# Sorted attention on one core: the second group's rows fetched between the rotations of the first group's queries, and gates and second latents in column groups of TensorE

## The chip, the core and the metric

One core of a Trainium2 chip runs the whole program. The metric is the device time of one execution in microseconds (us), as the median of several executions. The core has five engines that run beside each other, each with a queue of its own: TensorE (PE, matrix products; its weight loads are listed as PEld), VectorE (DVE), ScalarE (ACT), GpSimd (POOL) and SyncE (SP). In this kernel SP issues the plain DMA transfers, and POOL issues every indirect transfer (one whose rows are picked by a list of indices) besides arithmetic of its own.

## What is computed

Two layers on `x` of 16 x 256 tokens x 512, all in fp32, each an attention-like part and an ffn, each with a residual. Cut to what matters:

```python
x = x + L0_xattn(layernorm(x), k, fside_S2_0, ctx)   # long convolution, gated
x = x + L0_ffn(layernorm(x), ...)                    # 8 routed experts, top 2, and a shared one
x = x + L1_xattn(layernorm(x), ctx, itok, ...)       # latent attention
x = x + L1_ffn(layernorm(x), ...)                    # 512 -> 2048 -> gelu -> 512

# L0_ffn, the routing
logits = xf @ gate_w                                 # (tokens x 512) @ (512 x 8)
top_logits, top_idx = top_k(logits, 2)

# L1_xattn
q_c = q @ W_dq                                       # 512 -> 192 latents
q_nope = (q_c @ W_uq)                                # 16 heads of 128
q_rope = rope(q_c @ W_qr)                            # 16 heads of 64, rotated by position
scores = (q_nope . k_nope + q_rope . k_rope) * scale
good = (k_ids <= itok) & (k_ids >= itok - 8)         # 9 keys per token at most
out = softmax(where(good, scores, -1e30)) @ v @ W_o
```

There are 4096 tokens. Each token has an id `itok`, and it sees only the keys from `itok - 8` to `itok`.

## The kernel before

**Stages.** The kernel (class `Kernel`) runs five stages after each other: `conv_shared` (the convolution, the gate logits, the routing and the shared expert; PE ends it at about 982 us), `routed` (71 tiles of 128 rows through the routed experts, to about 1302 us), `attention_sorted` (to about 2260 us), `ffn` (to the end), and a fallback that isn't run on this input. A matmul in fp32 is recorded as two instructions ("passes").

**The convolution.** `conv_shared` loops over 32 rows, h = 0 to 31, with two convolution halves in each. A half is 20 passes of 512 columns (`y`, L292), which DVE multiplies with the context (`pr`, L297) and reduces (`oT`, L304). For each row `turn_inputs` transposes the values on PE (`pvt`, L258) into a PSUM buffer that the row before has used, and so it waits until DVE's products of that row (`kv`, 4 per half, `product`, L274) are done; PE turns the result (`po`, L316, and `xT`/`xt`, L317). Everything else of the stage is hung in between by four lists of steps per half (`one`, `mid`, `two`, `end`), which a schedule written by hand keeps in this order on PE, DVE and ACT. Four rows make one group of 512 tokens (`T4`, q = h % 4). At q = 0 the group that was completed a row before gets its gate logits: `logits` (L375, matmul at L380) is hung in `end`, and computes for each of 4 token tiles the product of 4 slices of `xT` (128 x 128, the stationary side) with a slice of `w_gate` (128 x 8, the moving side). That is 16 matmuls of 8 columns, or 32 passes, in each of 7 groups (h = 4, 8, ..., 28); the last group of tokens follows behind the loop, by the same function. At q = 1 DVE picks the two best experts from them (`tops`). On DVE the sort of the tokens by id also runs in this stage (`ranks`, L639 to L644, at h = 3 to 18).

**Sorted attention.** The tokens, sorted by key id, are cut into 32 tiles of 128, T = 0 to 31, and these into 8 groups of four (g = T // 4, t = T % 4). What a tile needs is spread over these functions:

- `fetch` brings a tile's rows of x (`xt`) and of the rotation's sines and cosines (`rr`), `fetch_routed` its two rows of routed experts (`yt`, twice), and `fetch_keys` its windows of keys (`gw`, 4 times). All are indirect DMAs that POOL issues (`fetch_rows`, L1727).
- `tokens` adds the two `yt` to `xt` on DVE (L1407 to L1410), normalizes (`layernorm`: L66, L68 on DVE, L70 and L71 on POOL, `xh` at L72 on DVE), and turns `rr` and `xh` on PE (L1416; `pt`, L99; copied by ACT at L100).
- `latents` (L1424) computes the 192 latents of a group of 512 tokens: two products of 128 latents each, `q0` (0 to 127) and `q1` (128 to 191, which stand in `q1` twice, in its lower and in its upper 64 lines, since the weights hold these 64 columns twice), 4 matmuls of 512 columns each, copied by ACT (L1428).
- `heads` is called 4 times per group, for 2 pairs of heads each time: products with `q0`, then with `q1` (L1439 to L1450), then the rotation: ACT swaps halves (`sw`, L1455), DVE multiplies by one factor (L1457), POOL multiplies and adds (L1458, L1459).
- `window` turns the keys on PE (`pkw` L1472, `prw` L1477) and makes the mask on DVE; `scores` (L1500, L1506), `weigh` and `weights` (DVE, with Exp on ACT) and `values` (`pu`, L1544) are the attention itself; `project` multiplies by W_o (`po`, 32 passes, L1560), DVE adds it to `xt` (L1565), and POOL sends the tile off (`x3s`, L1566).

PE's results `pq`, `pqr`, `pqn`, `pkw`, `prw`, `pu`, `po`, `prr` and `pt` share 7 PSUM buffers (tag `m`) in turn. `xt` has 8 buffers, `yt` and `rr` have 4, `gw` has 3.

The main loop, T = 0 to 33, works on tile T and, beside it, prepares the next group: its rows are fetched at t = 0 and 1, its `tokens` follow at t = 0 (tile 0), 1 (tile 1) and 2 (tiles 2 and 3), and at t = 3 come its `latents` and all 4 `heads`. `values` runs one tile behind, `project` two tiles behind. `tc.issue_after(i)` around calls keeps what they issue behind instruction `i` in the order in which the scheduler lays out each engine's queue; before, the one place it names in this stage is `first`, the last normalization of the first group's tokens.

The lines that the change touches are L328 to L329 (`w_gate`), L362 to L384 (`logits`), L745 (where it is hung), L1420 to L1428 (`latents`), L1430 to L1463 (`heads`), L1570 to L1578 (the start of sorted attention) and L1588 to L1629 (the loop's fetches and tokens).

Of the kernel before, what the change touches and what calls it, by code (L numbers as in the profile page):

```python
# [10 lines left out]
F32 = mybir.dt.float32  # L11
I32 = mybir.dt.int32
AF = mybir.ActivationFunctionType
ALU = mybir.AluOpType
# [4 lines left out]
P = 128  # L19
# [3 lines left out]
DC = D // P  # L23
EPS = 1e-5
E, EH, SH = 8, 256, 512
HEADS, HD, R = 16, 128, 64
KVC, QC = 128, 192
# [15 lines left out]
class Kernel:  # L43
# [59 lines left out]
    def conv_shared(self, x1d, xgd):  # L103
        nc, tc, a = self.nc, self.tc, self.a
        with ExitStack() as ctx:
# [4 lines left out]
            wp = pool("ab_w", 1)  # L110
# [214 lines left out]

            def load_shared_weights():
                w = {}
                w["gate"] = wp.tile([P, DC, E], F32, name="w_gate")  # L328
                nc.sync.dma_start(w["gate"], a["gate_w"].rearrange("(c p) e -> p c e", p=P))  # L329
                w["sw1"] = wp.tile([P, DC, SH], F32, name="w_s1")  # L330
                nc.sync.dma_start(w["sw1"], a["sw1"].rearrange("(c p) h -> p c h", p=P))
                w["sb1"] = wp.tile([P, SH // P], F32, name="b_s1")
                nc.sync.dma_start(w["sb1"], a["sb1T"])
                w["sw2"] = wp.tile([P, SH // P, D], F32, name="w_s2")
                nc.sync.dma_start(w["sw2"], a["sw2"].rearrange("(c p) d -> p c d", p=P))
                return w

            def load_experts(c):
# [20 lines left out]
                rows_of, pattern=[[ROOM, E]], base=0, channel_multiplier=0,  # L359
                allow_small_or_imprecise_dtypes=True,  # L360
            )
            T4 = 4  # L362

            def put(index, src):
# [10 lines left out]
            def logits(st, t0, n):  # L375
                xT = st["xT"]
                pl = ps_t.tile([P, n, E], F32, tag="t", name="pl")
                for t in range(n):
                    for c in range(DC):
                        nc.tensor.matmul(  # L380
                            pl[:, t, :], xT[:, c, (t0 + t) * P : (t0 + t + 1) * P], st["w"]["gate"][:, c, :],
                            start=(c == 0), stop=(c == DC - 1),
                        )
                return {"h": st["h"] + t0, "n": n, "pl": pl}  # L384

            def tops(r):

# [327 lines left out]
            w = None  # L715
# [3 lines left out]
            with tc.manual_schedule(engines=order):  # L719
                for h in range(HC):  # L720
# [19 lines left out]
                    if before is not None:  # L740
                        st = before
                        if q == 0:
                            if older is not None:
                                mid.append(lambda: outs(older, 3))
                            end.append(lambda: st.update(r=logits(st, 0, T4)))  # L745
                        elif q == 1:
                            steps = tops(st["r"])
                            one = {k: [steps[k]] for k in range(3)}
                            mid.append(lambda: hidden(st, 0))
                            end += [lambda: rank_rows(st["r"]), lambda: hidden(st, 1)]  # L750
                        elif q == 2:
                            one = {0: [lambda: slots(st["r"])], 1: [lambda: shares(st["r"])]}
                            mid.append(lambda: hidden(st, 2))
                            end.append(lambda: hidden(st, 3))
                        else:
                            mid.append(lambda: outs(st, 0))
                            end += [lambda: outs(st, 1), lambda: outs(st, 2)]
                        if q >= 2:
                            for t in (2 * q - 4, 2 * q - 3):
                                end += [lambda t=t: send(st["r"], t), lambda t=t: send_route(st["r"], t)]  # L760
# [587 lines left out]
    def attention_sorted(self, fetched, ygd, x3s, end_of_queries):  # L1348
# [8 lines left out]
        with ExitStack() as ctx:  # L1357
# [60 lines left out]
                self.transposed(st["xT"][:, :, toks], xh, ps_m, "m")  # L1418

            def latents(st):  # L1420
                for n, lo in (("q0", 0), ("q1", P)):
                    pq = ps_m.tile([P, N], F32, tag="m", name="pq")
                    for c in range(DC):
                        nc.tensor.matmul(  # L1424
                            pq, wdq[:, c, lo : lo + P], st["xT"][:, c, :], start=(c == 0), stop=(c == DC - 1)
                        )
                    st[n] = tp.tile([P, N], F32, tag=n, name=n, bufs=1)
                    nc.scalar.copy(st[n], pq)  # L1428

            def heads(st, two):  # L1430

                q0, q1 = st["q0"], st["q1"]
                pairs = (2 * two, 2 * two + 1)
                lo, hi = slice(0, QC - P), slice(QC - P, P)
                both = (lo, hi)
                pqr = [ps_m.tile([P, N], F32, tag="m", name="pqr") for hp in pairs]
                pqn = [[ps_m.tile([P, N], F32, tag="m", name="pqn") for i in range(2)] for hp in pairs]
                for k, hp in enumerate(pairs):
                    nc.tensor.matmul(pqr[k], wqr0[:, hp * P : (hp + 1) * P], q0, start=True, stop=False)  # L1439
                for k, hp in enumerate(pairs):  # L1440
                    for i in range(2):
                        nc.tensor.matmul(pqn[k][i], m0[:, 2 * hp + i, :], q0, start=True, stop=False)

                for k in range(2):
                    rr = both[k]
                    nc.tensor.matmul(pqr[k], wqr1[rr, two, :], q1[rr, :], start=False, stop=True)
                for k, hp in enumerate(pairs):
                    for i in range(2):
                        rr = both[i]
                        nc.tensor.matmul(pqn[k][i], m1[rr, hp, :], q1[rr, :], start=False, stop=True)  # L1450
                by_chunk = lambda t: t.rearrange("p (c q) -> p c q", q=CQ)
                for k, hp in enumerate(pairs):
                    sw = ap_.tile([P, N], F32, tag="sw", name="sw", bufs=3)
                    for i in range(2):
                        nc.scalar.copy(sw[both[i], :], pqr[k][both[1 - i], :])  # L1455
                    to = qr[:, :, hp * CQ : (hp + 1) * CQ]
                    nc.vector.tensor_tensor(to, by_chunk(pqr[k]), by_chunk(st["rope"][:, 0, :]), ALU.mult)  # L1457
                    nc.gpsimd.tensor_tensor(sw, sw, st["rope"][:, 1, :], ALU.mult)  # L1458
                    nc.gpsimd.tensor_tensor(to, to, by_chunk(sw), ALU.add)  # L1459
                for k, hp in enumerate(pairs):  # L1460
                    for i in range(2):
                        c0 = i * P // 2 + hp * CQ
                        nc.scalar.copy(qn[:, :, c0 : c0 + CQ], by_chunk(pqn[k][i]))  # L1463

            wins = {}

# [101 lines left out]
            new = lambda g: {"g": g, "y": []}  # L1568
            NG = NT_ // T4
            state = {0: new(0)}  # L1570
            for t in range(T4):
                fetch_routed(state[0], t)
                tokens(state[0], t)
            first = self.normed
            latents(state[0])
            window(0)
            for two in range(HP // 2):
                heads(state[0], two)  # L1578
            ats, uts = {}, {}
            for T in range(NT_ + 2):  # L1580
                g, t = T // T4, T % T4
                if T < NT_:
                    if 3 <= T + 2 < NT_:
                        fetch_keys(T + 2)
                    s = scores(state[g], T)
                    e = weigh(T, s)
                    nxt = state.setdefault(g + 1, new(g + 1)) if g + 1 < NG else None
                    if nxt is not None and t < 2:  # L1588
                        with tc.issue_after(first):
                            fetch((g + 1) * T4 + 2 * t)  # L1590
                            fetch_routed(nxt, 2 * t)
                    if nxt is not None and t == 3:
                        latents(nxt)
                if 1 <= T <= NT_:
                    uts[T - 1] = values(T - 1, ats.pop(T - 1))
                if T < NT_:
                    ats[T] = weights(e)
                    if T + 1 < NT_:
                        window(T + 1)
                    if nxt is not None and t == 3:  # L1600
                        for two in range(HP // 2):
                            heads(nxt, two)
                if T >= 2:
                    project(state[(T - 2) // T4], T - 2, uts.pop(T - 2))
                if T == NT_:
# [11 lines left out]
                        self.layernorm(xh, xt, small)  # L1617
                        self.transposed(xT[:, :, k * P : (k + 1) * P], xh, ps_m, "m")
                if T < NT_ and nxt is not None:
                    if t == 0:  # L1620
                        with tc.issue_after(first):
                            fetch((g + 1) * T4 + 1)
                            fetch_routed(nxt, 1)
                    for k in ((0,), (1,), (2, 3), ())[t]:
                        tokens(nxt, k)
                    if t == 1:
                        with tc.issue_after(first):
                            fetch((g + 1) * T4 + 3)
                            fetch_routed(nxt, 3)  # L1629
            return ahead  # L1630
# [261 lines left out]
```

## Time and profile before

| what | value |
|---|---|
| median of 3 timed executions | 3186.18 us (3185.9 to 3187.29) |
| the profiled execution, its own time | 3162.05 us |
| its span, from the first to the last instruction | 3159.9 us |
| mean granted TensorE clock | 0.987 |
| costliest PE groups: convolution L292, project L1560, ffn L1692, ffn L1680 | 572.2, 445.7, 442.0, 385.7 us |
| DVE: pr L297, reduce L304, product L274 | 174.6, 175.6, 174.0 us |
| POOL: indirect fetches of yt, of gw | 71.5, 133.2 us |
| bytes moved | 201.45 MB, 63 GB/s over the span |

The span is cut by the profile into 40 slices of 79 us; in each the PE digit is 9 (90% busy or more), except the first and the last slice (8) and the two around the start of sorted attention, at 1264 to 1422 us (7 and 8). The granted clock has the digit 9 in all but two slices (8, the same two around the start of sorted attention). The chain of work that ended last is followed back only over a last transfer, and holds 0% of the span, so it doesn't tell what bounds the middle. The costliest groups list no idle time of PE above 1.0 us in front of any of their lines: the idle time of PE is spread over small places.

In a line of the timeline the first number is the start in us from the span's start, the second the time, then engine, line, operation, destination and sources, tile shape and count; the bracket holds the idle time ahead of it and what ended it. In a line of the windows view the columns are the window and its length, the busy time of each engine with its number of instructions, the granted clock, the DMA share and the rate in GB/s.

### The profile page before, as it was taken

The page shows a single profiled execution, that of the slowest core. Times are in us where ns is not written, and L with a number is a line of the kernel's source. Part 1 is how long each engine was busy: PE and PEld are TensorE (multiplying, and loading weights), DVE is VectorE, ACT ScalarE, POOL GpSimd, SP SyncE. Part 2 cuts the span into 40 slices and gives each one's busy share as a digit, 9 for nine tenths or more (in the row PEclk, how much of TensorE's full clock was granted, in tenths as well). Part 3 has the DMA queues.
Part 4 walks back from the last instruction along what each step waited for, and adds up shares of the span by engine and source line. Part 5 has one row for each costly group of instructions (what it writes and reads, how often), then busy time and mean ns, then how long its engine had stood idle before and what let it go on. Part 6 is the DMA issues. An engine that isn't in the chain of part 4 may idle for free. (4 is left out here: it accounts for less than half of the span.)

```text
span 3159.9 us, 34421 instructions
## 1 busy us (share of the span) xinstructions
PE 3087.4 (98%) x12953; PEld 1577.1 (50%) x12953; DVE 1243.7 (39%) x2391; ACT 620.9 (20%) x1166; POOL 880.1 (28%) x1198
## 2 busy tenths in 40 slices
PE   8999999999999999789999999999999999999998
PEld 4455555545555666444454455455444444444443
DVE  6777777677664444433343243333200010000000
ACT  1111111111111111234323333332101101101100
POOL 2233233132125000455645554542210110111000
PEclk9999999999999999889999999999999999999999
DMA  4232122222118543311221121112300000000000
GB/s 115 68 111 85 51 71 62 49 71 62 38 46 243 167 140 130 119 41 43 62 81 46 49 88 48 50 48 71 117 10 10 20 27 13 14 27 20 7 14 15
DMA packets 120110, 201.45 MB, mean 64 GB/s; under 512 B 33352, under 2 KB 53224, under 8 KB 119296
## 3 DMA queue, kind: packets, MB, share of 16 engines
q1 hardware_dynamic: 91648, 117.24, 12.4%
q0 software_dynamic: 28288, 81.92, 8.1%
q8 instruction: 106, 1.74, 0.2%
q14 instruction: 68, 0.56, 0.1%
HBM read 131.73 MB, written 67.37 MB: 63 GB/s over the span
## 5 line engine op out<-in xcount | busy, mean ns | idle before, releaser
L292 PE MATMUL y<-kv,ut 128*128 128x512 f32 x1280 | 572.2, 603 | 0.6 <-DVE pr L297 0.6
L1560 PE MATMUL po<-nw,w 128*128 128x512 f32 x1024 | 445.7, 593 | 0.0
L1692 PE MATMUL po<-p,ht 128*128 128x512 f32 x1024 | 442.0, 592 | 0.0
L292 PEld LDWEIGHTS y<-kv,ut 128*128 128x128 f32 x1280 | 246.2, 194 | 301.2 <-issue 291.3
L1680 PE MATMUL ph<-xT,w 128*128 128x512 f32 x896 | 385.7, 592 | 0.0
L1692 PEld LDWEIGHTS po<-p,ht 128*128 128x128 f32 x1024 | 193.8, 190 | 237.9 <-issue 237.9
L1560 PEld LDWEIGHTS po<-nw,w 128*128 128x128 f32 x1024 | 192.3, 190 | 234.8 <-issue 229.3
L1680 PEld LDWEIGHTS ph<-xT,w 128*128 128x128 f32 x896 | 170.5, 190 | 214.0 <-issue 214.0
L1685 ACT ACTIVATE ht<-ph,p1b 128x512 f32<-128x512 f32 x128 | 87.9, 687 | 743.4 <-PE ph L1680 743.4
L297 DVE TENSOR_TENSOR pr<-y,cT 128x512 f32<-128x512 f32 x256 | 174.6, 682 | 140.0 <-PE y L292 139.7
L72 DVE TENSOR_SCALAR xh<-xt,ln_mv,ln_rs 128x512 f32<-128x512 f32 x60 | 34.0, 577 | 411.0 <-PE pt L99 339.8
L304 DVE TENSOR_REDUCE oT<-pr 128x64 f32<-128x512 f32 x256 | 175.6, 686 | 8.8
L274 DVE TENSOR_TENSOR kv<-pvt,cT 128x512 f32<-128x512 f32 x256 | 174.0, 680 | 0.0
L1727 POOL DMA_INDIRECT yt<-ygd,slot_s x64 | 71.5, 1118 | 294.8 <-DMA pre<-in_W_uvT_dram 239.7
L1727 POOL DMA_INDIRECT gw<-kvd,keys_of x128 | 133.2, 1041 | 62.1 <-issue 37.1
L1697 DVE TENSOR_TENSOR xt<-xt,po 128x512 f32<-128x512 f32 x28 | 19.3, 688 | 309.9 <-PE po L1692 296.8
L267 POOL TENSOR_TENSOR xt<-xt,sk 128x512 f32<-128x512 f32 x32 | 40.7, 1273 | 344.8 <-DVE sk L266 304.2
L870 PE MATMUL phg<-w,xTg 128*128 x568 | 134.6, 380 | 1.0 <-DVE xTg L860 0.9
L889 PE MATMUL pog<-w,hT 128*128 x284 | 133.7, 593 | 0.0
L1671 POOL TENSOR_TENSOR xt<-xt,p2b 128x512 f32<-128x512 f32 x28 | 37.0, 1332 | 340.2 <-DVE xh L72 339.5
L1457 DVE TENSOR_TENSOR w<-pqr,rope 128x512 f32<-128x512 f32 x64 | 44.2, 691 | 213.5 <-ACT sw L1455 213.5
L466 PE MATMUL ph<-xT,w_s 128*128 128x512 f32 x256 | 118.2, 607 | 0.0
(263 smaller groups left out, 3704.1 us busy)
## 6 DMA issues: line engine op xcount, KB each, us to landing
xg<-xgd SPq DMA_DIRECT2D x71, 256.0 KB, 2.7
ygd<-y SPq DMA_DIRECT2D x71, 256.0 KB, 2.2
xt<-in_x_dram SPq DMA_DIRECT2D x32, 256.0 KB, 3.4
ct<-in_ctx_dram SPq DMA_DIRECT2D x32, 256.0 KB, 3.5
ut<-in_kt_dram SPq DMA_DIRECT2D x32, 256.0 KB, 2.6
w<-in_w_dram SPq DMA_DIRECT2D x8, 1024.0 KB, 5.5
x1d<-xt SPq DMA_DIRECT2D x32, 256.0 KB, 2.8
x3s<-xt POOLq DMA_DIRECT2D x32, 256.0 KB, 3.7
```

The lines of the kernel that those rows point to most:

```text
L274: nc.vector.tensor_tensor(c["kv"][half][:, mc, :].rearrange("p (b j i) -> p b j i", i=NH, j=NH), c["vt"][:, mc, cols].rearrange("p (b i) - ...
L292: c["conv"] = nc.tensor.matmul(y, ut[:, (lc - mc) * P : (lc - mc + 1) * P], kv[:, mc, :], start=(mc == 0), stop=(mc == lc),).ins
L297: nc.vector.tensor_tensor(pr, y.rearrange("p (b j i) -> p b j i", i=NH, j=NH), cT[:, lc, cols].rearrange("p (b i) -> p b i", i=NH) .unsque ...
L304: nc.vector.tensor_reduce(c["oT"][:, lc, cols].rearrange("p (b j) -> p b j", j=NH), pr, AX.X, ALU.add)
L466: nc.tensor.matmul(ph, w["sw1"][:, c, f * P : (f + 1) * P], xT[:, c, :], start=(c == 0), stop=(c == DC - 1),)
L870: nc.tensor.matmul(ph, xT[:, c, :], w1[:, c, bass.ds(e * EH, EH)], start=(c == 0), stop=(c == DC - 1))
L889: nc.tensor.matmul(po, hT[:, q, :], w2[:, bass.ds(e * (EH * D // P) + q * D, D)], start=(q == 0), stop=(q == EH // P - 1),)
L1560: nc.tensor.matmul(po, ut[:, n].rearrange("p a j q -> p (a j q)"), nw[:, 2 * hp + i, :], start=(n == 0), stop=(n == HEADS - 1),)
L1680: nc.tensor.matmul(ph, w1[:, c, f * P : (f + 1) * P], st["xT"][:, c, :], start=(c == 0), stop=(c == DC - 1),)
L1685: nc.scalar.activation(ht, ph, AF.Gelu, bias=b1[:, f : f + 1])
L1692: nc.tensor.matmul(po, st["ht"][f][:, t * P : (t + 1) * P], w2[:, f, :], start=(f == 0), stop=(f == NF - 1),)
L1727: self.nc.gpsimd.indirect_dma_start(out=dst, out_offset=None, in_=src, in_offset=bass.IndirectOffsetOnAxis(ap=index, axis=0), bounds_check ...
```

## The change

It has four parts, in this order below.

1. *Gates.* `w_gate` is padded with zeros from 8 to 32 columns. A new function `parts`, hung in `mid` of the same half at q = 0, multiplies the group's 512 tokens by the 4 slices of the gates at once: the slice of the gates (128 x 32) is the stationary side now, and each of the 4 results goes to its own 32 rows of one PSUM tile `pg`, so to another column group of PE. ACT copies them to `g`. In `end`, where `logits` stood, `whole` sums the four by 4 matmuls of 8 columns with `picks`, four slices of the identity above each other, which are made once. The last group of tokens keeps `logits`.
2. *Second latents.* `q1` comes first and in two column groups: for 64 of PE's columns, the products with chunks 0 and 1, and for the other 64 with chunks 2 and 3. ACT copies both halves crosswise to `other`, and DVE adds. `q0` follows as before.
3. *Start of sorted attention.* The fourth tile's `yt` of the first group are fetched behind the first normalization, `window(0)` goes ahead of `latents`, and the second group's fetches of tiles 4 and 5 (`xt`, `rr`, `yt`, `yt` each) follow the last rotation of the second and the fourth call of `heads`.
4. *Later groups.* `heads` returns its last DVE and its last POOL instruction of the rotation (`turned`). In the loop the fetches of the next group's tiles stand behind `turned[1]`, and its `tokens` behind `turned[0]`, where both stood behind `first` before; that is, behind the rotations of the group before it.

```diff
@@ load_shared_weights
-                w["gate"] = wp.tile([P, DC, E], F32, name="w_gate")
-                nc.sync.dma_start(w["gate"], a["gate_w"].rearrange("(c p) e -> p c e", p=P))
+                w["gate"] = wp.tile([P, DC, 32], F32, name="w_gate")
+                nc.gpsimd.memset(w["gate"], 0.0)
+                nc.sync.dma_start(w["gate"][:, :, 0:E], a["gate_w"].rearrange("(c p) e -> p c e", p=P))
@@ conv_shared
+            picks = wp.tile([P, E], F32, name="picks")
+            nc.gpsimd.memset(picks, 0.0)
+            for c in range(DC):
+                nc.vector.tensor_copy(picks[c * 32 : (c + 1) * 32, :], self.ident[c * 32 : (c + 1) * 32, c * 32 : c * 32 + E])
...
+            def parts(st):
+
+                pg = ps_s.tile([P, T4 * P], F32, tag="s", name="pg")
+                for c in range(DC):
+                    nc.tensor.matmul(
+                        pg[c * 32 : (c + 1) * 32, :], st["w"]["gate"][:, c, :], st["xT"][:, c, :],
+                        start=True, stop=True, skip_group_check=True,
+                    )
+                st["parts"] = g = hp.tile([P, T4 * P], F32, tag="z", name="g")
+                nc.scalar.copy(g, pg)
+
+            def whole(st):
+                pl = ps_t.tile([P, T4, E], F32, tag="t", name="pl")
+                g = st.pop("parts")
+                for t in range(T4):
+                    nc.tensor.matmul(pl[:, t, :], g[:, t * P : (t + 1) * P], picks, start=True, stop=True)
+                return {"h": st["h"], "n": T4, "pl": pl}
...
-                            end.append(lambda: st.update(r=logits(st, 0, T4)))
+                            mid.append(lambda: parts(st))
+                            end.append(lambda: st.update(r=whole(st)))
@@ latents
-                for n, lo in (("q0", 0), ("q1", P)):
-                    pq = ps_m.tile([P, N], F32, tag="m", name="pq")
-                    for c in range(DC):
+                lo, hi = slice(0, QC - P), slice(QC - P, P)
+                pq = ps_m.tile([P, N], F32, tag="m", name="pq1")
+                half = DC // 2
+                for c in range(half):
+                    for r, k in ((lo, c), (hi, half + c)):
                         nc.tensor.matmul(
-                            pq, wdq[:, c, lo : lo + P], st["xT"][:, c, :], start=(c == 0), stop=(c == DC - 1)
+                            pq[r, :], wdq[:, k, P + r.start : P + r.stop], st["xT"][:, k, :],
+                            start=(c == 0), stop=(c == half - 1), skip_group_check=True,
                         )
-                    st[n] = tp.tile([P, N], F32, tag=n, name=n, bufs=1)
-                    nc.scalar.copy(st[n], pq)
+                other = tp.tile([P, N], F32, tag="xh", name="other")
+                for to, of in ((lo, hi), (hi, lo)):
+                    nc.scalar.copy(other[to, :], pq[of, :])
+                st["q1"] = tp.tile([P, N], F32, tag="q1", name="q1", bufs=1)
+                nc.vector.tensor_tensor(st["q1"], other, pq, ALU.add)
+                pq = ps_m.tile([P, N], F32, tag="m", name="pq")
+                for c in range(DC):
+                    nc.tensor.matmul(pq, wdq[:, c, 0:P], st["xT"][:, c, :], start=(c == 0), stop=(c == DC - 1))
+                st["q0"] = tp.tile([P, N], F32, tag="q0", name="q0", bufs=1)
+                nc.scalar.copy(st["q0"], pq)
@@ heads
-                    nc.vector.tensor_tensor(to, by_chunk(pqr[k]), by_chunk(st["rope"][:, 0, :]), ALU.mult)
+                    on_dve = nc.vector.tensor_tensor(
+                        to, by_chunk(pqr[k]), by_chunk(st["rope"][:, 0, :]), ALU.mult
+                    ).ins
                     nc.gpsimd.tensor_tensor(sw, sw, st["rope"][:, 1, :], ALU.mult)
-                    nc.gpsimd.tensor_tensor(to, to, by_chunk(sw), ALU.add)
+                    on_pool = nc.gpsimd.tensor_tensor(to, to, by_chunk(sw), ALU.add).ins
...
+                return on_dve, on_pool
@@ the start of sorted attention
-            for t in range(T4):
+            for t in range(T4 - 1):
                 fetch_routed(state[0], t)
+            tokens(state[0], 0)
+            with tc.issue_after(self.normed):
+                fetch_routed(state[0], T4 - 1)
+            for t in range(1, T4):
                 tokens(state[0], t)
-            first = self.normed
+            window(0)
             latents(state[0])
-            window(0)
+
+            state[1] = new(1)
             for two in range(HP // 2):
-                heads(state[0], two)
+                turned = heads(state[0], two)
+                if two % 2 == 1:
+                    with tc.issue_after(turned[1]):
+                        fetch(T4 + two // 2)
+                        fetch_routed(state[1], two // 2)
@@ the loop
-                    if nxt is not None and t < 2:
-                        with tc.issue_after(first):
+                    if nxt is not None and t < 2 and (g > 0 or t > 0):
+                        with tc.issue_after(turned[1]):
                             fetch((g + 1) * T4 + 2 * t)
                             fetch_routed(nxt, 2 * t)
...
                         for two in range(HP // 2):
-                            heads(nxt, two)
+                            turned = heads(nxt, two)
...
-                    if t == 0:
-                        with tc.issue_after(first):
-                            fetch((g + 1) * T4 + 1)
-                            fetch_routed(nxt, 1)
+                    if t == 0 and g > 0:
+                        fetch((g + 1) * T4 + 1)
+                        fetch_routed(nxt, 1)
                     for k in ((0,), (1,), (2, 3), ())[t]:
-                        tokens(nxt, k)
+                        with tc.issue_after(turned[0]):
+                            tokens(nxt, k)
                     if t == 1:
-                        with tc.issue_after(first):
+                        with tc.issue_after(turned[1]):
                             fetch((g + 1) * T4 + 3)
                             fetch_routed(nxt, 3)
```

More of the change, by code (lines that the diff above doesn't have):

```diff
@@ L380, in logits @@
                         nc.tensor.matmul(
-                            pl[:, t, :], xT[:, c, (t0 + t) * P : (t0 + t + 1) * P], st["w"]["gate"][:, c, :],
+                            pl[:, t, :], xT[:, c, (t0 + t) * P : (t0 + t + 1) * P], st["w"]["gate"][:, c, 0:E],
                             start=(c == 0), stop=(c == DC - 1),
```

## The prediction

> **What bounds the kernel now.** I read the page first, then the waits of TensorE (PE), then PE's timeline stage by stage, and the other engines' timelines only where PE stands still.
>
> ```profile
> PE 3087.4 (98%) x12953; PEld 1577.1 (50%) x12953; DVE 1243.7 (39%) x2391; ACT 620.9 (20%) x1166; POOL 880.1 (28%) x1198
> ```
>
> PE is busy 98% of the span, so an edit pays if it takes PE time away and costs if it makes PE wait. An fp32 matmul is two records ("passes") of 0.43 us at 512 columns. Three places matter. First the gates, with the timeline of PE at h = 4, h = 8 and h = 16:
>
> ```profile
> 126.42 0.66 PE L258 MATMUL pvt<-ident,vh 128*128 128x128 f32 x4 [3.57 <-DVE kv L274]
> ...
> 257.24 4.02 PE L380 MATMUL pl<-w_gate,xT 128*128 128x8 f32 x32
> 261.11 1.09 PE L316 MATMUL po<-ident,oT 128*128 128x128 f32 x4
> 262.00 11.31 PE L292 MATMUL y<-kv,ut 128*128 128x512 f32 x20
> ...
> 511.61 0.66 PE L258 MATMUL pvt<-ident,vh 128*128 128x128 f32 x4 [1.00 <-DVE kv L274]
> ```
>
> 32 passes of 8 columns take 3.5 to 3.9 us, and the convolution behind them 11.31 us where the usual one takes 8.75. The view of windows tells why:
>
> ```profile
> 262.00:265.00 3.00, 3.00 (x5) 1.35 (x5) 2.58 (x5) 0.00 (x0) 2.43 (x5) 0.50 0.16 48
> ```
>
> The granted clock (third from the end) is 0.50: so little work halves it. The convolution behind the gates takes 9.84 to 11.31 us in 6 of 7 groups. In the seventh (h = 16) it runs in 8.6, and pvt then waits 1.00 us for VectorE (DVE): DVE is the next limit. Second, the start of sorted attention:
>
> ```profile
> 1321.95 8.77 PE L1424 MATMUL pq<-xT,w_dq 128*128 128x512 f32 x16 [0.68 <-ACT xT L100]
> 1330.56 0.60 PE L1472 MATMUL pkw<-ident,gw 128*128 128x128 f32 x4
> ...
> 1347.53 2.08 PE L1439 MATMUL pqr<-q,w_qr 128*128 128x512 f32 x2 [6.95 <-DVE w L1457]
> ...
> 1391.90 2.09 PE L1544 MATMUL pu<-at,gw 32*128 32x128 f32 x32 [6.46 <-DVE at L1534]
> ```
>
> The second heads call waits 6.95 us, because DVE stands behind the second group's token work. Third, the steady groups, PE and then POOL:
>
> ```profile
> 1420.30 7.13 PE L1424 MATMUL pq<-xT,w_dq 128*128 128x512 f32 x16
> ...
> 1461.79 14.00 PE L1560 MATMUL po<-nw,w 128*128 128x512 f32 x32
> ...
> 1479.66 13.90 PE L1560 MATMUL po<-nw,w 128*128 128x512 f32 x32
> ```
>
> ```profile
> 1465.46 1.26 POOL L1459 TENSOR_TENSOR w<-w,sw 128x512 f32<-128x512 f32 x1
> 1476.81 0.64 POOL L1566 DMA_DIRECT2D x3s<-xt  x1 [10.09 <-DVE xt L1565]
> ```
>
> PE doesn't wait here at all. POOL ends its rotations at 1466.72 and is idle for 10.09 us. What used to be fetched before the rotations now stands in this gap.
>
> **Part 1, gates (7 groups).** Let T0 be the end of keys (257.24 at h = 8). *whole* is 4 matmuls of 8 columns: 8 passes at L380's 3.5/32 = 0.11 us, 0.9 us for 3.5. But L317, which opens DVE's next stretch, waits for DVE too. At h = 4, 8, 12, 16 the sort's ranks (L639 to L644) hold DVE until T0+3.5 (260.7 at h = 8), so L317 moves only from T0+4.2 (4.2 to 5.0) to T0+3.5. At h = 20, 24, 28 there are no ranks and L317 can start at T0+1.8. From L317 to the last kv product DVE is full, 13.4 us (498.19 to 511.6), and pvt waits for that: T0+16.9, or T0+15.2. PE's own work would be there at T0+14.0. Pvt came at T0 + 18.1, 19.8, 18.3, 17.6, 18.1, 18.1, 18.4. *parts* adds 4 matmuls of 32 columns side by side, 0.86 us and 0.1 for the change of tile shape, in six groups; at h = 4 it lies in the 3.57 us wait and may keep the clock up (1.2 of 1.75 us). The sum of gains is 1.2+1.2+1.9+0.4-0.3+1.9+1.9+2.2 = 10.4 us. ScalarE's copy of pg (0.6 us) lies beside PE, with ScalarE at 20%; uncovered it is 0.6 us per group.
>
> Against it stands the new wait of 2.9 us before pvt in four groups. The Trainium skill ("TensorE: Matmul & The Clock Gate", the HAM clock gate) says that the clock falls after an idle window of 3.4 us, so 2.9 us would cost nothing. The rows are stricter: L380's 3.5 us, not idle at all, dropped it 6 times in 7; waits of 1.66 and 1.87 us did not; two of 3.57 and 3.59 us did, and from pvt to keys then took 12.07 us for 10.32, 1.75 more. With the transposes behind it I take 3 in 4: 4 x 0.75 x 1.75 = 5.3 us (0 to 7). At the kernel's start four small DVE copies (picks) stand ahead of z, which psk waits for: at DVE's 0.15 to 0.2 us for small operations 0.6 us (0 to 0.8); the added memset, some 0.2 us like the others, hides in POOL's wait. Gates: 10.4 - 5.3 - 0.6, about **-5 us** (0 to -14).
>
> **Part 2, second latents.** Eight passes of 128 columns (3.44 us) become eight of 64 in two column groups. The nearest row is scores: 8 passes of 128 columns in four column groups stand 0.22 us apart (1418.40, 1418.64 in PE's timeline), a quarter of 8 x 0.107, so the groups run fully side by side. By it: 1.72 + 0.1, gain 1.62. The skill (same page, row/col tiling) measured three column tiles at 2.38 times, 0.79 of ideal; by that 2.17 us and a gain of 1.2. I take the row: 7 x 1.62 = **-11.3 us** in groups 1 to 7 (-8 to -12; nothing if they ran in turn). q0 comes last now; its copy (0.2 + 0.59) lies beside pu and window (1.11 + 0.93). The two more copies (0.58) and the add (0.69) precede the use of q1 by six full matmuls, 5.2 us.
>
> **Part 3, start of sorted attention.** Six yt fetches now stand ahead of the first token's L70 and not eight; by 1.3 us each and DVE's order the last xh comes about 0.9 us earlier. Then window goes ahead (1.8 us at the low clock), latents lose 1.7, and q0's copy is exposed (0.8 us). Heads start about 1.4 us earlier. The four heads calls take 4 x 8.12 = 32.5 us for 42.1 (1331.43 to 1373.54): -9.6. POOL keeps up: two calls are 10.5 us of rotations and 5.4 of the four fetches, 15.9 against 16.2. But in the built order VectorE's xh of token 4 stands ahead of the first weigh, and L71 for it behind four fetches after the last rotation (and a fifth between L70 and L71). From the end of heads: rotations +4.9, L71 +12.4; then DVE's rows up to at(0) sum to 11.8, so pu at +24.4, where it was +18.4. Sum -1.4 - 9.6 + 6.0 = **-5 us** (0 to -10).
>
> **Part 4, the fetches of groups 2 to 7.** The same rule (token work after the rotations) holds in each later group. Read in the built order: behind the last rotation POOL has xt, rr, yt, yt, rr, yt, yt, rr, yt, yt, L70, rr, L71, and only then x3s. DVE has this token's xh ahead of the add of project (L1565). The second project of the group takes the PSUM buffer that this add frees: seven tiles with tag m on, po, four pu, pkw, prw, then po. So PE waits for the add, the add stands behind xh, xh waits for L71, and that for ten fetches. From R = 1466.72: ten at 1.36 to 1.42 (duration and 0.3 of issue), then L70, rr, L71 as in 1330.47 to 1333.82: L71 ends at R+15.9; xh 0.6 and the add 0.7: PE goes on at R+17.3. It went on at 1479.66 = R+12.9. That is a new wait of 4.3 us (3.8 at the quickest pitch, to 4.8) in six groups. It is longer than both waits that dropped the clock, so 1.6 us more each (0 to 1.75). 6 x 5.9 = **+35 us** (23 to 39). The later chain holds: x3s, xt, gw end 4 us ahead of their windows.
>
> **Sum.** -5 - 11.3 - 5 + 35 = +14 us: the profiled execution's 3162.05 (span 3159.9) becomes 3176. The timed runs' median lies 24.1 above it; carried over, 3186.18 + 14 = **3200**.
>
> **The rivals.**
> *Faster: the new wait isn't there.* It decides at R+12.9: if ten fetches and L71 are through by R+11.6, at 1.0 us a fetch, which is the instruction alone without the 0.3 of issue, PE never waits. Then all else stands: 3186 - 21 = 3165. For it speaks that POOL has a 10 us gap; against it, every run of fetches in POOL's timeline keeps 1.3 or more. 0.15.
> *No change: the wait comes, the clock stays.* 6 x 4.3 = 26 against 21: 3191 at most, 3186 with the gates better. For it: at h = 16 the clock stayed. 0.17.
> *Slower still: column groups take turns.* Parts would cost 3.4 us and latents gain nothing: about 30 more, 3229. Against it the scores row. 0.06.
> The forecast has 0.62.
>
> **Numbers.** The likeliest's own range is 3190 to 3214. To 8 in 10: 3168 to 3216, which leaves out half of the first rival and the last. A change of 0.2%, 6.4 us, is what can be told from none. Slower 0.67 (nearly all of the forecast, a third of the second rival, the last), within 0.17, faster 0.16.
>
> **What would show it.** In the changed profile: L380's place with 8 passes and the convolution behind it at 8.7 us; pvt waiting 1 to 3 us for DVE kv; the latents at 5.4 us for 7.06; no wait in the second heads call; and po waiting for the add six times, about 4 us each. If po waits for nothing I am wrong in sign; if latents stay at 7 us, in part 2.

## The result, and the profile after

| comparison | before, us | changed, us | ratio (95%) |
|---|---|---|---|
| first | 3186.73 | 3208.82 | 1.0067 (1.0049 to 1.0084) |
| second (e9) | 3162.22 | 3170.99 | 1.0031 (1.0018 to 1.0043) |
| third (e12) | 3189.39 | 3211.20 | 1.0068 (1.0055 to 1.0081) |

The changed kernel is slower in all three. Executions came in two kinds, and each of the six comparisons of this document fell wholly into one: in four (on chips 1, 3, 11 and 12) the kernel before takes 3160 to 3162 us, the quicker kind; in two (the first, and the third on chip 15) 3187 to 3189, the slower kind. That the chip makes the kind is likely and not shown. The profiled execution from which the prediction was worked out (3162.05) is of the quicker kind, that of the changed kernel (3212.03, span 3210.3) of the slower. So the two first profiles, 50 us apart, can't be subtracted. The changed kernel was profiled again in the quicker kind (e9, span 3167.3); that is the one to hold against the profile of before.

First what answers to the lines shown of before, in the changed kernel's first profile: engines, then PE's timeline at h = 8, then at the latents of the second group (g = 1).

```profile
PE 3086.9 (96%) x12841; PEld 1565.2 (49%) x12841; DVE 1250.7 (39%) x2403; ACT 629.5 (20%) x1181; POOL 879.8 (27%) x1200
```

```profile
257.48 0.95 PE L407 MATMUL pl<-picks,g 128*128 128x8 f32 x8
258.29 0.64 PE L316 MATMUL po<-ident,oT 128*128 128x128 f32 x4
258.76 8.75 PE L292 MATMUL y<-kv,ut 128*128 128x512 f32 x20
...
274.26 0.92 PE L258 MATMUL pvt<-ident,vh 128*128 128x128 f32 x4 [2.88 <-DVE kv L274]
...
1437.39 1.94 PE L1451 MATMUL pq<-xT,w_dq 128*64 128x512 f32 x8
1439.26 3.70 PE L1462 MATMUL pq<-xT,w_dq 128*128 128x512 f32 x8
```

Eight passes stand where 32 stood, the convolution behind them runs in 8.75 us for 11.31, and pvt now waits 2.88 us for DVE. The second latents (L1451) take 1.9 us for 3.5 (half of the 7.13 at L1424 before). Then the steady group, on the second profile (e9), PE first, then POOL, then DVE:

```profile
1447.96 14.00 PE L1599 MATMUL po<-nw,w 128*128 128x512 f32 x32
1461.89 0.43 PE L1539 MATMUL ps<-w,kn 128*32 128x128 f32 x8
...
1465.39 0.60 PE L1516 MATMUL prw<-ident,gw 128*128 128x128 f32 x4
1469.35 15.42 PE L1599 MATMUL po<-nw,w 128*128 128x512 f32 x32 [3.35 <-DVE xt L1604]
```

```profile
1451.63 1.26 POOL L1497 TENSOR_TENSOR w<-w,sw 128x512 f32<-128x512 f32 x1
1453.04 1.04 POOL L1775 DMA_INDIRECT xt<-x1d,order  x1
...
1465.09 1.00 POOL L1775 DMA_INDIRECT yt<-ygd,slot_s  x1 [0.30 <-issue]
1466.12 0.20 POOL L70 TENSOR_TENSOR ln_rs<-ln_mv,eps 128x1 f32<-128x1 f32 x1
1466.48 1.02 POOL L1775 DMA_INDIRECT rr<-roped,place  x1 [0.16 <-issue]
1467.52 0.59 POOL L71 TENSOR_TENSOR ln_rs<-ln_rs,mhalf 128x1 f32<-128x1 f32 x1
```

```profile
1468.15 0.55 DVE L72 TENSOR_SCALAR xh<-xt,ln_mv,ln_rs 128x512 f32<-128x512 f32 x1 [5.89 <-POOL ln_rs L71]
1468.61 0.68 DVE L1604 TENSOR_TENSOR xt<-xt,po 128x512 f32<-128x512 f32 x1
```

The brackets read as a chain backwards: the second project (po, 1469.35) waits for the add (1468.61), which stands behind xh on DVE, which waited 5.89 us for L71 on POOL, which stands behind the fetches that follow the last rotation (1451.63). The page of the same profile, whose last two columns are the idle time ahead of a group and who ended it:

```profile
L1599 PE MATMUL po<-nw,w 128*128 128x512 f32 x1024 | 458.3, 607 | 20.1 <-DVE xt L1604 20.1
```

20.1 us in six waits, and the 1024 matmuls are 12.6 us longer than before (445.7), because the clock falls at each wait. The view of windows, with the granted clock third from the end, just behind the wait and 6 us later:

```profile
1469.40:1472.40 3.00, 3.00 (x4) 1.40 (x5) 2.90 (x7) 0.20 (x1) 0.79 (x2) 0.53 0.23 87
1475.00:1478.00 3.00, 3.00 (x8) 1.33 (x7) 2.15 (x4) 0.00 (x0) 2.39 (x3) 1.00 0.31 100
```

In the changed kernel's first profile, and in e12's, the same six places look different. PE's timeline there:

```profile
1491.93 0.64 PE L1545 MATMUL ps<-w,krz 128*32 128x64 f32 x16
1492.98 0.43 PE L1539 MATMUL ps<-w,kn 128*32 128x128 f32 x5 [0.40 <-issue]
1493.72 0.30 PE L1539 MATMUL ps<-w,kn 128*32 128x128 f32 x2 [0.32 <-issue]
...
1495.16 0.33 PE L1545 MATMUL ps<-w,krz 128*32 128x64 f32 x5 [1.03 <-issue]
1496.59 0.45 PE L1545 MATMUL ps<-w,krz 128*32 128x64 f32 x4 [1.09 <-issue]
1498.01 0.34 PE L1545 MATMUL ps<-w,krz 128*32 128x64 f32 x2 [0.97 <-issue]
...
1503.02 14.04 PE L1599 MATMUL po<-nw,w 128*128 128x512 f32 x32
```

"issue" means that PE waited for nothing that the profile shows. The scores ahead of po trickle: 8.06 us for 1.97 (they are called standing scores below). When PE comes to po, the add has been done for 4 us (it ran at 1498.19), so po waits for nothing. The chain on POOL and DVE is the same as in e9, though: the add ends 16.6 us behind the last rotation (16.4 in e9), and po was due at 12.9 before the change. So the standing hides the wait and goes beyond it. Of the 43 us between this profile and e9's, 20.8 lie in the routed stage, 8.2 between it and the first project, where scores stand too, and 13.6 from there to the last project.

### The profile page after: what moved, and what is told of

It reads as the page before. It is cut to its first block, busy times and chain, and to the rows that moved or that the text cites. A ratio compares the mean times of both kernels' runs of the same rounds, so it can differ in the third digit from the quotient of the medians.

```text
span 3210.3 us, 34239 instructions
## 1 busy us (share of the span) xinstructions
PE 3086.9 (96%) x12841; PEld 1565.2 (49%) x12841; DVE 1250.7 (39%) x2403; ACT 629.5 (20%) x1181; POOL 879.8 (27%) x1200
## 5 line engine op out<-in xcount | busy, mean ns | idle before, releaser
L292 PE MATMUL y<-kv,ut 128*128 128x512 f32 x1280 | 563.3, 595 | 0.6 <-DVE pr L297 0.6
L895 PE MATMUL phg<-w,xTg 128*128 x568 | 136.4, 384 | 11.9 <-DVE xTg L885 10.9
```

Source lines behind the costliest of these rows:

```text
L292: c["conv"] = nc.tensor.matmul(y, ut[:, (lc - mc) * P : (lc - mc + 1) * P], kv[:, mc, :], start=(mc == 0), stop=(mc == lc),).ins
L895: nc.tensor.matmul(ph, xT[:, c, :], w1[:, c, bass.ds(e * EH, EH)], start=(c == 0), stop=(c == DC - 1))
```

## The experiments

All times are medians; the ratio is to the kernel before, run beside each.

| run | what it is | us | before, us | ratio (95%) |
|---|---|---|---|---|
| e1 | before again, one execution | 3162.06 | 3160.74 | |
| e2 | gates alone | 3156.62 | 3160.74 | 0.9987 (0.9980 to 0.9994) |
| e3 | gates and latents | 3145.72 | 3160.74 | 0.9954 (0.9940 to 0.9967) |
| e4 | e3 and the start | 3146.59 | 3160.74 | 0.9955 (0.9941 to 0.9968) |
| e5 | changed, add first | 3135.50 | 3160.69 | 0.9926 (0.9910 to 0.9943) |
| e6 | changed, run cut in two | 3157.73 | 3160.69 | 0.9995 (0.9987 to 1.0004) |
| e7 | changed, narrow rows | 3169.40 | 3160.69 | 1.0025 (1.0013 to 1.0036) |
| e8 | changed, plain fetches | 3136.77 | 3160.69 | 0.9928 (0.9911 to 0.9944) |
| e9 | changed again | 3170.99 | 3162.22 | 1.0031 (1.0018 to 1.0043) |
| e10 | e5, mixed gates | 3135.77 | 3159.51 | 0.9924 (0.9910 to 0.9937) |
| e11 | e5 again | 3136.73 | 3159.51 | 0.9927 (0.9913 to 0.9940) |
| e12 | changed, a third time | 3211.20 | 3189.39 | 1.0068 (1.0055 to 1.0081) |

**The kernel before again (e1).**

> The kernel before once more, for a second profile of it, since the first profiled execution (3162.05 us) lies 24 us under the median of its timed runs and the changed kernel's (3212.03) 3 us over its own. If that difference is one of executions, this profile spans some 3184 us, and the routed stage (from the first tile of experts to the last), which took 313.8 us in the first profile of before and 334.9 in that of the changed kernel, takes 330 to 336 here, with a stall of 10 us or more behind the twenty indirect fetches that POOL issues in it. If the change itself made the routed stage longer, it stays at 314 and the 24 us are somewhere else.

It spans 3160.0 us, and the routed stage takes 314.4 us (313.8 in its first profile). So a miss: this wasn't the slower kind of execution, and where before loses its 26 us there is not seen. But in e9 the changed kernel, too, has 314.1 us in that stage, so the 21 us more in its first profile come with the slower kind and not with the change alone.

**The change in parts (e2, e3, e4).**

> Only the gates of the change (parts and whole in place of the gate logits), all of attention as before. The sum of the prediction: -5 us (0 to -14); the profile of the changed kernel has the convolution 3.3 us shorter and the shared expert's end 1.7 us shorter, so -5. Rival, that the new waits of pvt for VectorE eat all of it: 0. The convolution behind the gates should run at 8.6 us, and pvt at h = 8, 12 and 16 wait 2 to 3.6 us.

> The gates and the second latents in column groups, with all fetches and token work of attention as before. By the sum -5 - 11.3 = -16 us against before, about 3170 us. If column groups took turns: -5. If the new order of the latents (q0 last) exposed a copy: up to 4 us less gain. Against the changed kernel it should be about 38 us faster, if the loss lies in the order of the fetches.

> Gates, second latents and the changed start of sorted attention (the second group's fetches between the rotations of the first one's queries), but the loop's fetches and token work of the later groups as before. By the prediction's sum the start is worth another -5 us (-21 in all); by the profile of the changed kernel, where the first two scores of the first group stand still for 9 and 5 us beside POOL's fetches, it is worth nothing or costs a few: 0 to +5 against the kernel with gates and latents alone. The first scores of groups 2 to 7 take 1.97 us here, and po never waits.

e3 takes e2 and the diff's `latents`; e4 is the changed kernel with the loop's order put back, by this and the same for the loop's two other places of fetches:

```diff
-                        with tc.issue_after(turned[1]):
+                        with tc.issue_after(first):
                             fetch((g + 1) * T4 + 2 * t)
...
-                        with tc.issue_after(turned[0]):
+                        with tc.issue_after(turned[0] if g == 0 else first):
                             tokens(nxt, k)
```

Gates: 3156.62 - 3160.74 = -4.1 us. Latents: 3145.72 - 3156.62 = -10.9 us. Without the loop's new order the kernel is faster than before, not slower, so the loss is in that order. The start adds nothing in e4: with the loop's fetches released early, POOL issues more of them ahead of the keys, gw starts at 1393.45 us (1383.04 in e5, where the heads begin 4.0 us earlier), and PE waits four times for it:

```profile
PE pkw L1511 <- DMA gw<-kvd,keys_of: 5.6, 4, 3.1
```

(the waits of PE in e4 from 1295 to 1450 us: in total, times, longest).

**Add first (e5, e11).**

> The changed kernel with one edge in VectorE's queue: in groups 2 to 7 the next group's first token work stands behind the add of the group's first project and no longer ahead of it, so that the second project's buffer comes free early; POOL's run of ten fetches stays. By the prediction (the second project waits for that add) it is about 35 us faster than the changed kernel. By the reading of the changed kernel's trace (the scores ahead of it take 8.1 us instead of 1.97 because TensorE runs short of instructions while POOL issues that run, and the add is done before po is reached) it gains nothing: within 5 us of the changed kernel, with the scores still at 8 us.

> The changed kernel with the add ahead of the token work once more, beside the one with mixed gates and beside new runs of the kernel before: 0.9926 of the time of before as in its first runs (0.991 to 0.9943), without any wait of po.

```diff
-                nc.vector.tensor_tensor(xt, xt, po, ALU.add)
+                adds.append(nc.vector.tensor_tensor(xt, xt, po, ALU.add).ins)
...
-                        with tc.issue_after(turned[0]):
+                        with tc.issue_after(adds[T - 3] if g > 0 and k == 0 else turned[0]):
                             tokens(nxt, k)
```

One added edge turns 1.0031 into 0.9926, and e11 repeats it (0.9927). In e5's timelines of DVE and PE the add now runs as soon as its project has ended, and po follows the windows without a wait (its line is cut off where the view ends):

```profile
1462.02 0.69 DVE L1604 TENSOR_TENSOR xt<-xt,po 128x512 f32<-128x512 f32 x1 [12.49 <-PE po L1599]
1462.62 1.53 DVE L1433 SCALAR_TENSOR_TENSOR xt<-yt,routes,xt 128x512 f32<-128x512 f32 x2
```

```profile
1465.41 0.60 PE L1516 MATMUL prw<-ident,gw 128*128 128x128 f32 x4
1465.85 4.46 PE L1599 MATMUL po<-nw,w 128*128 128x512 f32 x10
```

The fetches behind the last rotation are still there: POOL issues nine in a row, then x3s, then three more ahead of L70 and L71. The reading of the first trace alone (the standing scores, no wait at po) had said "no gain". It failed here, where no scores stand; e5 and e11 both ran in the quicker kind, so what the edge is worth in the slower one is not shown. From each group's last project to the next group's, five times running, it is now 111.68 us (116.6 to 118.3 in e9, 113.2 to 114.1 in e1).

**The run of fetches (e6, e7, e8).**

> The changed kernel with POOL's run of ten fetches behind the last rotation cut in two: four fetches, then the normalization of the first tile of tokens, then the other seven. The normalization then ends about 6.7 us after the last rotation instead of 15.5, so the add is no longer late. By the prediction (wait for the add) that is about 35 us faster than the changed kernel. By the reading of the trace, POOL still issues fetches until some 16 us after the last rotation, over the scores: they stay at 6 to 8 us and the gain is under 8 us.

> The changed kernel with the rows of the routed experts (yt) of groups 3 to 8 fetched at an eighth of their width (256 B instead of 2 KB, as many rows, as many fetches, from other places of the same table), spread over the full row by VectorE's operand; the output is not the reference's, since seven eighths of the rows are left out. The bytes in a run of ten fetches fall from 2.2 to 0.8 MB, POOL's instructions stay. If the traffic starves TensorE, the scores come down to 2 to 4 us, and the wait of po for the add shows (up to 4 us, as predicted). If POOL's issuing of indirect fetches does it, scores stay at 8 us, and the time with them.

> The changed kernel with the indirect fetches of xt, rr and yt of groups 3 to 8 replaced by plain transfers of as many rows and bytes, issued by POOL at the same places; the output is not the reference's, since the rows are not the picked ones. POOL's run behind the last rotation falls from 15.5 to 7 or 8 us. If the traffic starves TensorE, the scores still stand for 4 us or more. If the indirect fetches on POOL do it, the scores take 1.97 us and the kernel is 35 to 45 us faster than the changed one.

```diff
# e6: tokens of tile 0 ahead of the other tiles' fetches
+                    normed0 = self.normed if g > 0 else turned[1]
...
-                        with tc.issue_after(turned[1]):
+                        with tc.issue_after(turned[1] if t == 0 else normed0):
                             fetch((g + 1) * T4 + 2 * t)
# e7, w = 64 of 512 columns in groups 2 to 7
-                    self.fetch_rows(yt, ygd, self.slot_s[:, k, T : T + 1], NT * P)
+                    src = ygd if w == D else ygd.rearrange("n (c x) -> (n c) x", x=w)
+                    self.fetch_rows(yt[:, 0:w], src, self.slot_s[:, k, T : T + 1], NT * P)
# e8, in groups 2 to 7 (xt and rr alike)
+                        nc.gpsimd.dma_start(yt, ygd[T * P : (T + 1) * P, :])
```

(Their expectations call groups 2 to 7 "groups 3 to 8".) No scores stood in these three, so they say nothing of that; they do tell what the wait at po is made of. The waits of PE from 1440 to 2240 us, first e7, then e6:

```profile
PE po L1608 <- DVE xt L1613: 19.7, 6, 3.7
```

```profile
PE prw L1516 <- DVE xt L1604: 9.8, 6, 1.6
PE pu L1583 <- DVE at L1573: 9.3, 6, 1.8
PE pt L99 <- DVE xh L72: 0.5, 1, 0.5
```

e7 moves 0.8 MB for 2.2 in a run (by the shapes of its tiles), and the wait stays (19.7 us for 20.1): it isn't the bytes. e8 moves all the bytes with POOL's instructions at 0.6 us each for 1.3, and the wait is gone: it is the time in which POOL issues them. In e6 the wait left po, as the early normalization should do, and came back one tile later, in two places: on POOL seven fetches now stand ahead of x3s (issued at 1472.02, its add done at 1464.17), the second tile's fetch of xt waits for x3s, and on DVE the softmax's sums (which pu waits for) and the next add stand behind that tile's token work. So 11 of the 33 us that e5 wins are won, which is neither of the two expectations.

**The changed kernel again (e9, e12).**

> The changed kernel once more, beside new runs of the kernel before. In the runs so far the kernel before took 3161 us, against 3186 when it was first timed, and no scores stood still in any profile, with wide rows or narrow. If the standing scores (8.1 us) belong to the executions in which the kernel before takes 3186 us, and not to the change, they take 1.97 us here, and in their place po waits for VectorE's add 3.5 to 4.5 us in groups 2 to 7, as predicted; the time is then 3161 + 14 = 3175 us by the prediction's sum, or 3169 + a few by the kernel with narrow rows. If the standing scores belong to the change with full rows, they take 8 us here too, and the time is about 22 us over that of before.

> The changed kernel a third time, since its first two comparisons with the kernel before differ (1.0067 with standing scores in its profile, 1.0031 without). If standing scores are the exception, they take 1.97 us again, po waits for the add six times by 3.3 to 3.7 us, and the ratio is 1.002 to 1.004. If they come back, the ratio is near 1.0067 and po doesn't wait.

e9 has every wait that the prediction names and no standing scores; e12 has the standing scores at 8.0 to 8.2 us, no wait at po, and again 1.0068. So this is one kernel in two kinds of executions, and slower than before in both.

**Mixed gates (e10).**

> The changed kernel with the add ahead of the token work, and with the gates in column groups only at h = 4, 20, 24 and 28; at h = 8, 12 and 16, where the changed kernel's profile has pvt wait for VectorE and the clock fall behind it, the sixteen gate matmuls of before stand again. In the profiles the groups at h = 8, 12 and 16 took 1.2, 2.0 and 1.6 us more with column groups than without, the others 1.3 to 3.8 us less. If these sums hold, it is 4.8 us faster than the kernel with the add first and column groups everywhere. If the 16 short matmuls bring the clock drops of before back in full (up to 1.5 us each), the gain is 0 to 2 us.

```diff
-                            mid.append(lambda: parts(st))
-                            end.append(lambda: st.update(r=whole(st)))
+                            if h in (8, 12, 16):
+                                end.append(lambda: st.update(r=logits(st, 0, T4)))
+                            else:
+                                mid.append(lambda: parts(st))
+                                end.append(lambda: st.update(r=whole(st)))
```

In the profiles its last convolution matmul starts 3.1 us earlier than e11's (922.8 for 925.9); in the timed runs it is 1.0 us (0.9924 for 0.9927), which can't be told from none and lies in the second range expected (0 to 2), not at 4.8.

## Why the prediction was right

The forecast's case came in where its numbers came from, in the quicker kind of execution: slower, by a wait of project for the add in six groups. Its sum was +14 us; there it was +8.8. In the slower kind, in which the first comparison ran, it was +22, and that the forecast fits there is in part luck: po waited for nothing, which the prediction had named as the sign of a wrong direction, and the standing scores, which nobody forecast, stood in the wait's place (6 x 6.1 = 37 us, for the +35). What the prediction describes, an add that comes late for po, was there (16.6 us behind the last rotation), but hidden. The steps:

- **The new wait, +35.** Taking it away (e9 to e5, each by its own ratio: 1.0031 - 0.9926 = 0.0105 of 3161) gave 33 us; between the profiles of e9 and e5 the six groups differ by 33.7 us. The chain was as read out of the built order. With R = 1452.9 us (the end of the last rotation), L71 ends at R + 15.2 (R + 15.9 predicted) and PE goes on at R + 16.5 (R + 17.3), because the fetches ran at 1.30 us each where 1.36 to 1.42 was taken. So the wait is 3.35 us and not 4.3, but the clock and what follows cost 2.3 us a group and not 1.6: the clock was at half for 3.4 us around the end of the wait in four groups and for 6.8 in two. That the sum came to 33 for 35 is luck: two errors of nearly one size in opposite directions.
- **Gates, -5.** Measured -4.1 (-1.9 to -6.3). *parts* takes 1.06 us at h = 8 (0.96 predicted). pvt's wait came out at 2.87 us at h = 4, 8, 12 and 16 (2.9 predicted), and 1.22 at h = 20, 24, 28. The clock fell at all four of the long ones, not three; none of the three short ones dropped it. The Trainium skill ("TensorE: Matmul & The Clock Gate", the HAM clock gate) has the clock fall after an idle window of 3.4 us; here waits of 2.87 us, with transposes behind them, were enough four times, so the stricter reading of the rows holds.
- **Second latents, -11.3.** Measured -10.9. The two groups of columns run side by side: 1.94 us for eight passes, 5.5 for the whole. The row of the scores was the right neighbour.
- **Start, -5.** From the start of the last routed product to the first project: 100.3 us in e9 for 107.4 and 105.9 in the two profiles of before, so -5.6 to -7.1; the four heads calls run without a wait (1324.10 to 1356.5) and pu(0) starts 23.6 us after them (24.4 predicted). But it holds only with the loop's late fetches; in e4 it is worth nothing. Nor does it show in the slower kind, where the changed kernel takes 108.5 us from the one to the other.
- **Not in the sum.** From e3 to e5, the start and the late fetches without their wait gain 10.2 us, where 5 were put down. Some 3 us of this are in the later groups: e3 waits there four times for xh (2.9 us in all), e5 once (0.5). This is why the sum of +14 was too high: -4.1 - 10.9 - 10.2 + 33 makes +8.
- **The rivals.** "The wait isn't there" decided at 1.0 us a fetch; the pitch stayed at 1.3. "The clock stays" fell: it dropped six times in six. "Column groups take turns" fell with L1451.
- **The base.** The prediction carried +14 over to the median 3186. That the profile of before and that median lay 24 us apart was taken as a constant; it is the slower kind of execution, in which the change loses 13 us more. The +14 lies between what the two kinds give.

## What to carry to other kernels

Work that is moved behind an instruction takes a place in every queue it uses: here the fetches delayed a normalization on POOL, that a token's row on DVE, and that an add whose only fault was to stand behind it and hold a PSUM buffer. Before giving up such a change, look for the one edge that lets the freeing instruction go first: with it the change gains 0.74% in the quicker kind of execution, where alone it ran. And hold the profile's own time against the median before subtracting two profiles: a difference of 24 us in 3186 was larger than the whole effect.

## What the hardware showed that was not expected

In two of the twelve profiles of the changed kernel and its variants, and in none of the others, all other engines nearly stood still while POOL issued a long run of indirect fetches, and went on within 3 us of its end. In the routed stage of the changed kernel's first profile (twenty fetches, 984.91 to 1010.79 us), DVE ("remote": the view names no engine of this core as the releaser):

```profile
992.27 0.69 DVE L923 TENSOR_TENSOR y<-pog,e_b 128x512 f32<-128x512 f32 x1 [2.20 <-remote]
1000.86 0.42 DVE L899 COPY hs<-phg 128x256 f32<-128x256 f32 x1 [7.90 <-remote]
1005.08 0.29 DVE L1034 COPY m<-pm 128x128 f32<-128x128 f32 x1 [3.80 <-remote]
...
1012.05 0.69 DVE L885 COPY xTg<-ptg 128x512 f32<-128x512 f32 x1 [6.49 <-remote]
```

The same stage, with the same fetches, takes 313.8 us in the profile of before and 334.9 and 333.0 in these two. In sorted attention the six first scores took 8.0 to 8.2 us for 1.97, in steps of 0.7 to 1.4 us with a few matmuls in each; otherwise PE gets through 96 matmul records there in 1.97 us. The 23 of the 32 scores in each of these two profiles that have no indirect fetch over them take 1.97 to 1.98 us. Whether it needs a run of fetches is open: every fetch over a score there is part of a run or follows one within 1.4 us, and the single fetches over scores in the profiles of before (1.97 us all the same) ran in the quicker kind, where a run does nothing either. Whether the issuing or the bytes do it is open, too, since e7 and e8, which would tell it, ran where nothing stood; and the kernel before was not profiled in the slower kind, so that most of its own 26 us lie in the routed stage is likely and not shown.
